# A graph network of two layers with experts: block sizes at the end of the second layer, expert steps in the attention's last ticks, and the side of memory of one buffer pool

## The chip, the cores and the metric

The kernel runs on one core of a Trainium2 chip. Its engines are TensorE (PE, with weight loads shown apart as PEld), VectorE (DVE), ScalarE (ACT), GpSimd (POOL) and SyncE (SP, which issues most transfers here). The metric is the device time of one execution in microseconds; several runs are taken and the median is compared.

## The reference

Four stages follow one another. Each takes the layer norm of `x` and adds its result to `x`. There are N = 6250 nodes with D = 256 values each, and 106,250 edges sorted by destination.

```python
# L0_gnn: a message for every edge, the mean by destination, then a second projection
h = relu(concat([x[src], edge_attr], 1) @ W1 + b1)
agg = segment_sum(h, dst, N) / maximum(segment_sum(1, dst, N), 1)[:, None]
x = x + relu(concat([x, agg], 1) @ W2 + b2)

# L0_ffn: graph attention over 131,072 other edges and one loop per node gives a score for
# each of 4 experts; the best 2 are mixed
h = (x @ W_gat).reshape(N, 4 heads, 4 experts)
e = leaky_relu(a_src[src2] + a_dst[dst2]);  alpha = segment_softmax(e, dst2)
agg = segment_sum(h[src2] * alpha[..., None], dst2) + b_gat
scores = layernorm(agg).reshape(N, 4, 4).mean(1);  w = softmax(top_k(scores, 2))
x = x + sum over ei of gate[ei] * (gelu(x @ W1[ei] + b1[ei]) @ W2[ei] + b2[ei])   # 256 -> 512 -> 256

# L1_gnn: h squared is gathered, summed with edge weights, and its root taken
h = relu(x @ Wp.T + bp)
agg = sqrt(segment_sum(edge_weight[:, None] * (h ** 2)[src], dst, N))
x = x + h @ W1.T + b1 + agg @ W2.T + b2

# L1_ffn: one shared network of three layers, and the best 2 of 4 small ones (256 -> 128 -> 64 -> 256)
gates = softmax(x @ gW + gb);  topw = softmax(top_k(gates, 2))
x = x + shared(x) + sum of topw * expert(x)
```

(In every line on the right the layer norm of `x` stands for `x`.)

## The kernel before

**Data.** The nodes are cut in T = 49 tiles of 128. The tile `x_all` holds `x` for all nodes through the whole kernel, and `b_all` the transposed normalized values, which are the matmuls' moving operand. All data are 32-bit floats. Each engine works through its own instructions in the order in which the program writes them; the framework adds the waits. So the order of the Python code is the order of every engine, and the loops below interleave several pieces of work by hand. Pieces are written as Python generators: one call of `next` writes one step, up to the next `yield`.

**Memory pools.** Tiles come from pools, which are laid from the left end of the on-chip memory (SBUF) or, with `side="right"`, from its other end. A pool that is closed gives its place to pools opened later, and then the first use of the new tile waits for the last use of the old ones. `ea1` (L1285) holds three buffers of edge attributes of 6144 bytes a partition, filled by `load_attr` on the queue SP (L1304). It lies at the left end, at bytes 153,856 to 172,288 of each partition, and the scratch of layer 1 behind it. `w5` and `n5`, opened at the right end for the first experts, hold their weights (bytes 207,520 to 226,016) and their hidden and output values (195,232 to 207,520). They cover scratch of layer 1: its hidden values and projections (172,288 to 210,176) and its sums (210,176 to 222,532).

**Layer 1, edges.** Groups of six tiles of 128 edges: gathers of `y` rows by POOL (L1101), transposes of the attributes, a projection, sums over destinations by matmuls with 0/1 matrices.

**Attention with the first experts.** The attention's edges stand in 640 columns of 128, eight to a tick, so there are NA = 80 ticks, and a loop of NA + 5 in which a tick's gathering, scoring, weighing, spreading and adding are each one step behind the other. `experts1` (L1540) is a generator of 396 steps. A step is eight matmuls with 256 columns: the first or second half of a hidden layer (`first`, with the Gelu at L1593), or one node tile's output (`second`, L1609 and the store to DRAM at L1613). Its weights come by `load` (L948) and its bias by L1569, both through SP, in whose order small loads at L941, L948, L1569 and their neighbours stand ahead of them. Each tick calls `slot()` five times. A slot writes one expert step (`advance(layers, n)`), one step of each routing or node job that stands ready (`run(steps, False)`), the loads of expert outputs (`load_outputs`, L1941) and the start of new jobs (`start_steps`). The fifth slot gives an expert step in ticks 0 to 69 alone:

```python
                slot(int(k < 70))
```

By that the 396 steps are used up in tick 81 of 85.

**Drain.** As the sums of attention become final, `gates` (L1840) turns them into routing weights, a chain of small DVE and ACT operations (Sqrt, Exp); `node_values` (L1953) mixes the four experts' outputs, normalizes, transposes, projects, squares and writes the row of `hp_dram` that layer 2 gathers. The loop behind the ticks writes what is left of all of these. Where it interleaves, ACT has to load the table of a function that it did not use last (L1719 and others).

**Layer 2.** When `hp_dram` is written, POOL gathers 831 tiles of 128 edges (L1101, `hg`), in 139 groups of six. `weights_of` (L2386) makes the matrices of edge weights, `add_up` (L2402, L2407) sums by matmul into one PSUM tile a block. A block is a run of node tiles, at most BT = 4:

```python
        blocks = [(t, BT) for t in range(0, T - 5, BT)] + [(T - 5, 2), (T - 3, 1), (T - 2, 2)]
```

When a block's last edge is summed, `roots` takes the square roots (L2419), `end_of2` ends each of its node tiles (projection, norm, transposes, logits of the gate; L2228), `gates2` (L2256) ranks the experts and `experts2` (L2310) computes the shared network and the four small ones: 11 calls of `first`, `then` and the like for the whole block, then per node tile three PSUM tiles of outputs, which DVE adds to `x_all` with the gate's weights; a DMA at L2369 writes the block out. The main loop (L2431 to L2452) makes one pass a group: it issues the gathers of nine groups ahead, writes matrices and sums, up to two steps of `experts2`, a step of each tile's end, and in every second pass starts a new tile's end. Only past the last group does every pass start one. The logits of two blocks have room beside each other in `px` (`area`). Between the drain and the layer DVE sets constants: the ones behind `g2_0` and `g2_1` (L2198), the zeros of `nothing` (L2220), and the small tiles `lower`, `place` and `second` (L2206 to L2214), which `gates` has of its own (L1828 to L1837).

After layer 2 a few instructions check that the graph fitted the fixed layout, and a general version, which did not run here, would be used otherwise.

Of the kernel before, what the change touches and what calls it, by code (L numbers as in the profile page):

```python
# [8 lines left out]
F32 = mybir.dt.float32  # L9
# [832 lines left out]
def kernel(ctx: ExitStack, tc: tile.TileContext, a: dict, out: bass.AP):  # L842
# [71 lines left out]
    with ExitStack() as fast:  # L914
# [275 lines left out]

        att = fast.enter_context(tc.tile_pool(name="att", bufs=1))
        gate = att.tile([P, T, X], F32, name="gate")
        attention = fast.enter_context(ExitStack())
        gat = attention.enter_context(tc.tile_pool(name="gat", bufs=1))
        src2 = gat.tile([P, KA], I32, name="src2")
# [82 lines left out]
        with ExitStack() as layer:  # L1278
# [3 lines left out]
            order = srt.tile([P, KT], F32, name="order")  # L1282
            wp = layer.enter_context(tc.tile_pool(name="w1", bufs=1))
            wix = layer.enter_context(tc.tile_pool(name="wix", bufs=1))
            wea = layer.enter_context(tc.tile_pool(name="ea1", bufs=3))  # L1285

            def load_weights():
                return (
# [347 lines left out]
        def advance(queue, n):  # L1636
            for _ in range(n):
                if queue and next(queue[0], queue) is queue:
                    queue.pop(0)
# [3 lines left out]
        with (  # L1643
# [180 lines left out]
                    )  # L1824
                    V.tensor_add(acc[:, :, at], acc[:, :, at], rest)


            lower = n2.tile([P, X, X], F32, name="lower")  # L1828
            V.memset(lower, 0.0)
            for k in range(1, X):  # L1830
                V.memset(lower[:, k, 0:k], 1.0)
            place = n2.tile([P, X], F32, name="place")
            for k in range(X):
                V.memset(place[:, k : k + 1], float(X - 1 - k))
            second = n2.tile([P, 2], F32, name="second")
            V.memset(second[:, 0:1], 0.0)
            V.memset(second[:, 1:2], 1.0)  # L1837
            bg = bcast_row(n2, "bg", a["L0_ffn_b_gat_T"])
            gamma = bcast_row(n2, "gamma", a["L0_ffn_ln_gamma_T"])
            beta = bcast_row(n2, "beta", a["L0_ffn_ln_beta_T"])  # L1840
# [246 lines left out]
                    steps.append([node_values(ws), False])  # L2087

            def slot(n=1):
                advance(layers, n)  # L2090
                run(steps, False)
                load_outputs()
                start_steps()
# [5 lines left out]
            def complete(t1):  # L2099

                while ends and ends[0] <= t1:
                    waiting.append((passed[0], ends[0] - passed[0]))
                    passed[0] = ends.pop(0)

            passed = [0]
            last_columns = list(range(KB, KT, G))
            counted = False
            for k in range(NA + 5):
                if k < NA:
                    fetch(k)  # L2110
                if k == 1:
                    own_edges()
                now, here, there, before = k - 2, k - 3, k - 4, k - 5
                if 0 <= before < NA:
                    add_up(before, 0)
                slot()
                if now in range(NA):
                    score(now, 0)
                slot()
                if here in range(NA):  # L2120
                    weigh(here)
                tables()
                if there in range(NA):
                    spread_out(there, 0)
                run(routing, False)
                slot()
                if 0 <= before < NA:
                    add_up(before, 1)
                slot()
                if now in range(NA):  # L2130
                    score(now, 1)
                run(routing, False)
                slot(int(k < 70))
                if there in range(NA):
                    spread_out(there, 1)
                for _ in range(2):
                    if last_columns:
                        count_last(last_columns.pop(0))
                if not last_columns and not counted:
                    routing.append([last_edges(), False])  # L2140
                    counted = True
                if counted and 0 <= before < NA:
                    complete(near_blocks(before + 1)[0] if before + 1 < NA else T)
            while layers or steps or routing or waiting or done["begun"] < T:
                slot()
                tables()
                run(routing, False)
# [4 lines left out]


        BT = 4
        blocks = [(t, BT) for t in range(0, T - 5, BT)] + [(T - 5, 2), (T - 3, 1), (T - 2, 2)]
        with (
            tc.tile_pool(name="w8", bufs=1, side="right") as wp,
            tc.tile_pool(name="e7", bufs=2) as wk,
# [36 lines left out]
            )  # L2195
            g2s = [wp.tile([EH2 + 1, NX, BT, P], F32, name=f"g2_{i}") for i in range(2)]
            for g2 in g2s:
                V.memset(g2[last, :, :, :], 1.0)  # L2198

            NQ = BT * NX  # L2200
            px = psx.tile([P, P + 8 * NQ], F32, name="px")
            lanes = px[:, 0:P]
            V.tensor_copy(lanes, lane)

            lower = wp.tile([P, NX, NX], F32, name="lower")
            V.memset(lower, 0.0)  # L2206
            for k in range(1, NX):
                V.memset(lower[:, k, 0:k], 1.0)
            place = wp.tile([P, NX], F32, name="place")
            for k in range(NX):  # L2210
                V.memset(place[:, k : k + 1], float(NX - 1 - k))
            second = wp.tile([P, 2], F32, name="second")
            V.memset(second[:, 0:1], 0.0)
            V.memset(second[:, 1:2], 1.0)  # L2214

            def area(at, n):
                return px[:, P + at : P + at + n]

            nothing = wp.tile([P, BT * P], F32, name="nothing")
            V.memset(nothing, 0.0)  # L2220

            def end_of2(b, i, root):


                w = blocks[b][0] + i
                pm = psm.tile([P, D], F32, name="pt")
                mm(pm, lambda c: root[:, i, :], lambda c: w2t, 1)
                V.tensor_add(x_all[:, w, :], x_all[:, w, :], pm)  # L2228
                st = wk.tile([P, 6], F32, name="ln_st")
                V.bn_stats(st, x_all[:, w, :])  # L2230
                mv = wk.tile([P, 2], F32, name="ln_mv")
                V.bn_aggr(mv, st)
                rs = wk.tile([P, 1], F32, name="ln_rs")
                V.tensor_scalar(rs, mv[:, 1:2], EPS, None, op0=OP.add)
                SC.activation(rs, rs, AF.Sqrt)
                yield
                V.reciprocal(rs, rs)
                off = wk.tile([P, 1], F32, name="off")
                V.tensor_scalar(off, mv[:, 0:1], rs, -1.0, op0=OP.mult, op1=OP.mult)
                xn = wk.tile([P, D], F32, name="xn")  # L2240
                SC.activation(xn, x_all[:, w, :], AF.Identity, bias=off, scale=rs)
                yield
                transposed(psm, b_all[:, w, :], xn)
                yield
                pg = psm.tile([P, D], F32, name="pt")
                mm(pg[:, 0:NX], lambda c: b_all[:, w, c * P : (c + 1) * P], lambda c: gw[:, c, :])
                V.tensor_add(area(b % 2 * NQ + i * NX, NX), pg[:, 0:NX], gb)

            def gates2(b):


                t0, n = blocks[b]
                q = n * NX
                s = area(b % 2 * NQ, q).rearrange("p (n k) -> p n k", k=NX)
                m = wk.tile([P, BT], F32, name="m")[:, :n]
                V.tensor_reduce(m, s, axis=AX.X, op=OP.max)  # L2256
                V.tensor_sub(s, s, m.unsqueeze(2).to_broadcast([P, n, NX]))
# [44 lines left out]
                    gate[:, t0 : t0 + n, :], pick.rearrange("p n i k -> p n k i"),  # L2302
                    axis=AX.X, op=OP.add,
                )

            def experts2(b):

# [32 lines left out]
                for e in range(NX):  # L2340
                    if e + 1 < NX:
                        first(e + 1)
                        yield
                    then(e)
                    yield
                for i in range(n):
                    t = t0 + i
# [71 lines left out]
                SC.activation(root, pe, AF.Sqrt)  # L2419
                return [(b, i, root) for i in range(n)]  # L2420

            complete, ends, coming, routes, layers = [], [], [], [], []
            ended = [0] * len(blocks)
            AHEAD = 9
            for k in range(AHEAD):
# [3 lines left out]
            while k < len(groups2) or complete or coming or ends or routes or layers:  # L2429
                if k + AHEAD < len(groups2):  # L2430
                    fetch(k + AHEAD)  # L2431
                if k + 1 < len(groups2):
                    weights_of(k + 1)
                if k < len(groups2):
                    add_up(k)
                advance(layers, 1)
                for item in list(ends):
                    if next(item[1], ends) is ends:
                        ends.remove(item)
                        b = item[0]  # L2440
                        ended[b] += 1
                        if ended[b] == blocks[b][1]:
                            routes.append(gates2(b))
                            layers.append(experts2(b))
                if coming and (k % 2 or k >= len(groups2)):
                    b, i, root = coming.pop(0)
                    ends.append((b, end_of2(b, i, root)))
                while complete:
                    coming += roots(complete.pop(0))
                advance(routes, 1)  # L2450
                advance(layers, 1)
                k += 1  # L2452


# [69 lines left out]
```

## Time and profile before

| what | value |
|---|---|
| median of 3 runs | 3698.01 us (3695.89 to 3698.55) |
| profiled execution | 3697.09 us, its span 3695.1 us |
| mean granted clock of TensorE | 0.897 |
| busy: PE / PEld / DVE / ACT / POOL | 3433.4 / 2766.9 / 2199.3 / 1406.3 / 2252.5 us |
| POOL's gathers for the attention (L1101, `sg`) | 640, 612.7 us |
| POOL's gathers for layer 2 (L1101, `hg`) | 831, 784.1 us |
| expert matmuls of the attention stage (L1088, `ph` and `py`) | 1600 and 1568, 386.8 and 384.8 us |

The profile is of one execution, so its sums belong to its own 3697.09 us. A busy time is that of all instructions of an engine; instructions that only issue a transfer, wait or branch are not counted. The granted clock is the share of full speed that TensorE had, and a matmul's duration stretches with it. A row of the timeline names the engine, the line of the kernel, the operation, `out<-in` by the program's names, and in brackets the idle time ahead with what released it. A mean over the span hides that the stages have different limits, so stretches of the span are read apart.

### The profile page before, as it was taken

What the parts mean: (1) busy time and instruction counts of PE and PEld (TensorE: products, weight loads), DVE (VectorE), ACT (ScalarE), POOL (GpSimd) and SP (SyncE); (2) the same over time, 40 slices, a digit from 0 to 9 for tenths busy, and PEclk for the clock granted to TensorE, in tenths of its full rate; (3) what the DMA queues carried; (4) which work ended last, traced back from release to release, by engine and by line L of the source; (5) the groups of instructions that cost most, each with busy time, mean ns of one, the idle gap of its engine ahead of it and who ended that gap; (6) DMA issues with size and microseconds to landing.
All of it is one profiled execution on the core that took longest, in us unless ns stands there. A gap on an engine that the chain in (4) does not pass through costs nothing. (4 is left out here: it accounts for less than half of the span.)

```text
span 3695.1 us, 54304 instructions
## 1 busy us (share of the span) xinstructions
PE 3433.4 (93%) x18495; PEld 2766.9 (75%) x18495; DVE 2199.3 (60%) x6073; ACT 1406.3 (38%) x2714; POOL 2252.5 (61%) x2364
## 2 busy tenths in 40 slices
PE   7899999999999999899999999996678889888898
PEld 3678888888888887788888888895455566666675
DVE  9999984444444444687757576877233444444445
ACT  4444444444444443334544454654011222211214
POOL 0466666666666664666655555560777777777771
PEclk9999999999999999999999999997557776776668
DMA  5456656656555553443534343543222222222221
GB/s 170 131 173 177 181 174 175 181 177 176 176 177 179 173 176 111 124 96 89 133 82 125 81 125 86 144 93 88 53 53 59 59 59 59 59 59 59 59 59 29
DMA packets 298963, 428.30 MB, mean 116 GB/s; under 512 B 101495, under 2 KB 208774, under 8 KB 298679
## 3 DMA queue, kind: packets, MB, share of 16 engines
q1 hardware_dynamic: 201254, 244.98, 22.0%
q0 software_dynamic: 89408, 178.08, 19.1%
q8 instruction: 150, 2.46, 0.3%
q10 hardware_dynamic: 8016, 1.68, 0.2%
q14 instruction: 135, 1.10, 0.1%
HBM read 382.05 MB, written 42.49 MB: 115 GB/s over the span
## 5 line engine op out<-in xcount | busy, mean ns | idle before, releaser
L1101 POOL DMA_INDIRECT yg<-y_dram,src x882 | 854.3, 969 | 590.2 <-issue 225.8
L1101 POOL DMA_INDIRECT hg<-hp_dram,src x831 | 784.1, 944 | 339.6 <-issue 235.2
L1101 POOL DMA_INDIRECT sg<-gat_dram,src x640 | 612.7, 957 | 402.3 <-DVE px L1729 170.0
L1088 PE MATMUL ph<-w1b,et 128*128 128x256 f32 x3528 | 835.3, 380 | 0.0
L1088 PEld LDWEIGHTS ph<-w1b,et 128*128 128x128 f32 x3528 | 636.8, 190 | 68.5
L2407 PEld LDWEIGHTS pe<-eq,hg 128*128 128x128 f32 x1984 | 398.8, 272 | 282.8 <-issue 141.6
L2407 PE MATMUL pe<-eq,hg 128*128 128x96 f32 (+10 forms) x1984 | 447.3, 364 | 161.3 <-DMA hg<-hp_dram,src 127.1
L1406 DVE TENSOR_TENSOR yg<-ph,yg 128x512 f32<-128x512 f32 x441 | 303.6, 688 | 384.5 <-PE ph L1088 381.9
L1088 PE MATMUL ph<-b_all,w 128*128 128x256 f32 (+1 forms) x1600 | 386.8, 381 | 11.2 <-DMA w<-in_L_ffn_W_dram 11.2
L1088 PE MATMUL py<-w,hh 128*128 128x256 f32 x1568 | 384.8, 384 | 7.7 <-ACT hh L1593 7.7
L1411 ACT ACTIVATE h<-yg 128x512 f32<-128x512 f32 x441 | 276.6, 628 | 293.1 <-DVE yg L1406 280.9
L2386 DVE TENSOR_SCALAR eq<-px,dst,ew 128x96 f32<-128x96 f32 x831 | 256.9, 369 | 175.3 <-PE pe L2407 123.6
L1083 ACT ACTIVATE et<-pt 128x512 f32<-128x512 f32 x441 | 262.5, 596 | 240.6 <-PE pt L1082 229.4
L1088 PEld LDWEIGHTS ph<-b_all,w 128*128 128x128 f32 x1600 | 291.8, 191 | 44.1 <-issue 11.3
L1088 PEld LDWEIGHTS py<-w,hh 128*128 128x128 f32 x1568 | 287.1, 190 | 42.5 <-ACT hh L1593 10.1
L1593 ACT ACTIVATE hh<-ph,b 128x256 f32<-128x256 f32 (+1 forms) x400 | 166.2, 466 | 296.7 <-PE ph L1088 295.8
L1082 PE MATMUL pt<-ident,ea 128*128 128x128 f32 x1764 | 269.5, 275 | 3.3 <-ACT et L1083 3.3
L1757 PE MATMUL po<-pp,B 128*128 128x240 f32 (+10 forms) x1280 | 254.9, 338 | 2.5 <-DVE B L1745 1.6
L1082 PEld LDWEIGHTS pt<-ident,ea 128*128 128x128 f32 x1764 | 213.9, 143 | 48.1 <-issue 19.4
L1757 PEld LDWEIGHTS po<-pp,B 128*128 128x128 f32 x1280 | 217.3, 191 | 15.2 <-issue 1.7
L1088 PE MATMUL py<-ew,g 65*128 65x256 f32 x392 | 165.7, 555 | 0.3 <-DVE some L2476 0.3
L1736 DVE TENSOR_TENSOR pp<-px,A 128x960 f32<-128x960 f32 (+10 forms) x160 | 156.0, 975 | 3.6 <-PE po L1757 3.3
(337 smaller groups left out, 4456.1 us busy)
## 6 DMA issues: line engine op xcount, KB each, us to landing
ea<-in_edge_attr_dram SPq DMA_DIRECT2D x147, 768.0 KB
y<-y SPq DMA_DIRECT2D x196, 128.0 KB
w<-in_L_ffn_W_dram SPq DMA_DIRECT2D x48, 512.0 KB
y<-ys SPq DMA_DIRECT2D x96, 256.0 KB
rb<-low_dram SPq DMA_DIRECT2D x80, 256.0 KB
yg<-y_dram,src POOLq DMA_INDIRECT x882
hg<-hp_dram,src POOLq DMA_INDIRECT x831
sg<-gat_dram,src POOLq DMA_INDIRECT x640
```

Of the source, the lines that this page charges most:

```text
L1082: TE.transpose(pt[:, c, :], src[:, c * P : (c + 1) * P], ident)
L1083: SC.activation(dst, pt.rearrange("p c k -> p (c k)"), AF.Copy)
L1088: TE.matmul(dst, lhs(c), rhs(c), start=c == 0, stop=c == n - 1)
L1101: GP.indirect_dma_start(out=dst, out_offset=None, in_=table[0:NP, :], in_offset=IndirectOffsetOnAxis(ap=idx, axis=0),)
L1406: V.tensor_add(y, ph, y)
L1411: SC.activation(h[:, j : j + 2, 0:D], y, AF.Relu)
L1593: SC.activation(hidden[u][:, f, :n, :], ph[:, f - f0, :n, :], AF.Gelu, bias=b1[:, e, f : f + 1],)
L1736: V.tensor_tensor(pps[g, half][:, :, 0:n, :], pay[:, js, :].unsqueeze(2).to_broadcast([P, HG, n, HV]), near[g][:, js, 0:n].unsqueeze(3).to ...
L1757: TE.matmul(po.rearrange("p b v -> p (b v)"), B[:, j, :], pp[:, j, 0:n, :].rearrange("p b v -> p (b v)"), start=half == 0 and j == 0, stop ...
L2386: V.tensor_scalar(equals[k][:, j, :], lanes[:, 0:NW], dst_of[:, t : t + 1], ew[:, t : t + 1], op0=OP.is_equal, op1=OP.mult,)
L2407: TE.matmul(sums[b][:, lo - t0 * P : hi - t0 * P], hg[:, j, :], eq[:, j, lo - n0 : hi - n0], start=False, stop=after >= (t0 + n) * P,)
```

## The change

Three things are changed.

First, `ea1` goes to the right end of the memory, at bytes 205,696 to 224,128. What lay behind it at the left end moves down by 18,432 bytes. The weights of the first experts then lie over `ea1` (and a table of counts) instead of layer 1's scratch, and their hidden and output values over layer 1's sums.

Second, slots: a slot gives an expert step if its `n` is not zero and the tick is below 80, or if it is the first of its tick, or if it lies in the loop behind the ticks. The fifth slot gives one in ticks 0 to 61 instead of 0 to 69. Counted from the loop: ticks 62 to 69 give four steps instead of five, tick 80 one instead of four, ticks 81 to 84 one each; 387 of the 396 are written by the end of the ticks and nine in the loop behind.

Third, layer 2. Blocks: ten of 4, then three of 2 (from tiles 40, 42 and 44) and three of 1 (46, 47, 48); before, eleven of 4, then 2, 1 and 2. A pass of the main loop writes up to three steps of `experts2` instead of two, and a tile's end is started in every pass once the tiles are those of the small blocks. As a block's `experts2` can now be ahead of its `gates2`, its outputs are held back until the routing is written, and the logits of four blocks have room. The ones and zeros of `g2` and `nothing` are set by POOL instead of DVE, and `lower`, `place` and `second` once, at the start, for both layers.

```diff
@@ in the pool att, ahead of layer 1
+        lower = att.tile([P, X, X], F32, name="lower")
+        V.memset(lower, 0.0)
+        for k in range(1, X):
+            V.memset(lower[:, k, 0:k], 1.0)
...
+        second = att.tile([P, 2], F32, name="second")
...
-            wea = layer.enter_context(tc.tile_pool(name="ea1", bufs=3))
+            wea = layer.enter_context(tc.tile_pool(name="ea1", bufs=3, side="right"))
...
             def slot(n=1):
-                advance(layers, n)
+                if n and (k < NA or k == NA + 5 or slots[0] % 5 == 0):
+                    advance(layers, n)
+                slots[0] += 1
                 run(steps, False)
...
-                slot(int(k < 70))
+                slot(int(k < 62))
...
+            k = NA + 5
             while layers or steps or routing or waiting or done["begun"] < T:
                 slot()
...
-        blocks = [(t, BT) for t in range(0, T - 5, BT)] + [(T - 5, 2), (T - 3, 1), (T - 2, 2)]
+        small = T - T % BT - 2 * BT
+        blocks = [(t, BT) for t in range(0, small, BT)]
+        blocks += [(t, 2) for t in range(small, T - 3, 2)] + [(t, 1) for t in range(T - 3, T)]
...
-                V.memset(g2[last, :, :, :], 1.0)
+                GP.memset(g2[last, :, :, :], 1.0)
...
-            px = psx.tile([P, P + 8 * NQ], F32, name="px")
+            px = psx.tile([P, P + 10 * NQ], F32, name="px")
...
+            def logits(b):
+                n = blocks[b][1] * NX
+                return area((0, NQ, 8 * NQ, 9 * NQ)[b % 4], n)
...
-            V.memset(nothing, 0.0)
+            GP.memset(nothing, 0.0)
...
+                routed.add(b)        # at the end of gates2
...
+                while b not in routed:   # in experts2, ahead of the outputs
+                    yield
...
-                if coming and (k % 2 or k >= len(groups2)):
+                if coming and (k % 2 or coming[0][0] * BT >= small):
...
                 advance(routes, 1)
-                advance(layers, 1)
+                advance(layers, 2)
```

More of the change, by code (lines that the diff above doesn't have):

```diff
@@ L1192 @@
         gate = att.tile([P, T, X], F32, name="gate")
+        lower = att.tile([P, X, X], F32, name="lower")
+        V.memset(lower, 0.0)
+        for k in range(1, X):
+            V.memset(lower[:, k, 0:k], 1.0)
+        place = att.tile([P, X], F32, name="place")
+        for k in range(X):
+            V.memset(place[:, k : k + 1], float(X - 1 - k))
+        second = att.tile([P, 2], F32, name="second")
+        V.memset(second[:, 0:1], 0.0)
+        V.memset(second[:, 1:2], 1.0)
         attention = fast.enter_context(ExitStack())
@@ L1825, in last_edges @@
                     V.tensor_add(acc[:, :, at], acc[:, :, at], rest)
[L1828 to L1837, printed above, removed]
             bg = bcast_row(n2, "bg", a["L0_ffn_b_gat_T"])
@@ L2103, in complete @@
                     passed[0] = ends.pop(0)
-            passed = [0]
+            passed, slots = [0], [0]
             last_columns = list(range(KB, KT, G))
@@ L2197 @@
             for g2 in g2s:
-                V.memset(g2[last, :, :, :], 1.0)
+                GP.memset(g2[last, :, :, :], 1.0)
             NQ = BT * NX
-            px = psx.tile([P, P + 8 * NQ], F32, name="px")
+            px = psx.tile([P, P + 10 * NQ], F32, name="px")
             lanes = px[:, 0:P]
             V.tensor_copy(lanes, lane)
[L2205 to L2214, printed above, removed]
             def area(at, n):
                 return px[:, P + at : P + at + n]
+            def logits(b):
+                n = blocks[b][1] * NX
+                return area((0, NQ, 8 * NQ, 9 * NQ)[b % 4], n)
             nothing = wp.tile([P, BT * P], F32, name="nothing")
-            V.memset(nothing, 0.0)
+            GP.memset(nothing, 0.0)
             def end_of2(b, i, root):
@@ L2246, in end_of2 @@
                 mm(pg[:, 0:NX], lambda c: b_all[:, w, c * P : (c + 1) * P], lambda c: gw[:, c, :])
-                V.tensor_add(area(b % 2 * NQ + i * NX, NX), pg[:, 0:NX], gb)
+                V.tensor_add(logits(b)[:, i * NX : (i + 1) * NX], pg[:, 0:NX], gb)
             def gates2(b):
@@ L2253, in gates2 @@
                 q = n * NX
-                s = area(b % 2 * NQ, q).rearrange("p (n k) -> p n k", k=NX)
+                s = logits(b).rearrange("p (n k) -> p n k", k=NX)
                 m = wk.tile([P, BT], F32, name="m")[:, :n]
@@ L2420, in roots @@
                 return [(b, i, root) for i in range(n)]
-            complete, ends, coming, routes, layers = [], [], [], [], []
+            complete, ends, coming, routes, layers, routed = [], [], [], [], [], set()
             ended = [0] * len(blocks)
```

## The prediction

> **What bounds the kernel now.** The page first: TensorE is nominally busy for nearly the whole span, so that figure decides nothing. The busy times by stretch do (their columns: stretch, its length, busy time of PE, weight loads, DVE, ACT and POOL with instruction counts, granted clock, DMA share, GB/s).
>
> ```profile
> PE 3433.4 (93%) x18495; PEld 2766.9 (75%) x18495; DVE 2199.3 (60%) x6073; ACT 1406.3 (38%) x2714; POOL 2252.5 (61%) x2364
> ```
>
> ```profile
> 1457.00:1489.10 32.10, 15.40 (x70) 12.18 (x68) 16.79 (x70) 6.40 (x14) 4.96 (x6) 0.75 0.21 44
> 2381.00:2533.00 152.00, 148.71 (x1100) 134.23 (x1096) 110.92 (x327) 87.91 (x159) 71.14 (x74) 0.99 0.42 93
> 2533.00:2547.20 14.20, 0.00 (x0) 0.00 (x0) 12.93 (x50) 2.50 (x6) 0.00 (x0) 0.50 0.70 190
> 2533.00:2580.70 47.70, 20.90 (x85) 14.16 (x85) 37.91 (x146) 18.81 (x47) 0.00 (x0) 0.68 0.45 124
> 3500.00:3618.00 118.00, 112.04 (x428) 88.96 (x427) 54.30 (x195) 21.17 (x38) 89.23 (x95) 0.64 0.23 62
> 3620.40:3687.10 66.70, 65.03 (x279) 42.69 (x277) 39.29 (x169) 36.57 (x74) 0.00 (x0) 1.00 0.05 16
> ```
>
> There are six stages. Edges, layer 1, to 1457: PE full. A gap to 1489: PE idle 16.7 of 32.1 us. Attention with experts to 2533: PE full at clock 0.99, DVE 73%. A drain to 2580.7: a serial chain, PE idle for its first 14.2 us. Layer 2: POOL issues 831 gathers at a pitch of 1.247 us (0.94 busy, 0.30 issue), 1036 us that nothing here alters. A tail from 3620.4, where the last sum is taken, to 3687.1: PE 65.0 of 66.7 us at clock 1.00; 8 us of output and end follow. The change touches the gap, the drain and the tail.
>
> **Gap: attribute buffers at the right end.** The timeline of the queue SP and of PE:
>
> ```profile
> 1302.85 126.35 SPq L1304 DMA_DIRECT2D ea<-in_edge_attr_dram  x15
> 1479.02 0.35 SPq L941 DMA_DIRECT2D bg<-in_L_ffn_b_gat_T_dram  x1
> 1483.59 2.56 SPq L948 DMA_DIRECT2D w<-in_L_ffn_W_dram  x2
> 1489.13 5.83 PE L1088 MATMUL ph<-b_all,w 128*128 128x256 f32 x16 [11.19 <-DMA w<-in_L_ffn_W_dram]
> ```
>
> SP has nothing to do from 1429 to 1479, yet the experts' first weights are issued at 1483.6. Their buffers share memory with layer 1's scratch, whose last user is the final node's projection at 1478.9. After the change those addresses are held by the edge attributes, last read at 1456.8. Issue to use took 1489.1 - 1483.2 = 6 us, so expert steps could start at 1463. All 16.7 idle us lie behind that, and the first 16 matmuls took 5.83 us where 1.73 us for 8 is usual: 2.4 us more. So the gain is at most 19 us, and 0 if SP's order keeps the weights behind its nine small loads. Against the full 19: the hidden activations overlie layer 1's sums (read until 1469.8), and attention's first score matmul, now at 1509.75, has its rows only at 1498.5, so it moves up 11 us. I take -12. PE is full for the next 1040 us, which carries it on. Expert steps that come between layer 1's last four PE steps can delay the attention's gathers by 4 x 1.73 = 7 us; 640 gathers at 1.247 are 798 us of that 1040, which covers it. Uncovered it would be 7.
>
> **Drain: fewer expert steps.** The experts take 396 steps of 1.73 us (8 matmul passes; 0.87 for the first halves of the single tile 48). Before, they end in tick 81 of 85. After, ticks 62 to 69 give four instead of five, tick 80 one instead of four, ticks 81 to 84 one each: 387 are issued by the end, and nine (seven full, two half: 13.8 us) go into the loop behind. As PE bounds these ticks, the last attention sum comes 14 us earlier (10 if DVE's 73% begins to bind, 17 if the ticks' waits fill too). The nine must then lie beside the drain. It has 26.8 us of idle PE, so the time itself is covered; uncovered it would be 13.8. Their outputs go by DRAM to nodes 44 to 48: the last store lands some 3 us after the last step, about where attention ended before, and those sums begin at 2555 now; with the drain 12 earlier that is still 7 us of slack.
>
> Not covered is ScalarE's table. Four of the nine steps use Gelu among Sqrt and Exp, two loads each:
>
> ```profile
> 2498.18 0.23 ACT L1719 ACTIVATE z<-z 128x32 f32<-128x32 f32 x1
> 2498.43 1.28 ACT L1593 ACT_TABLE_LOAD   x1
> ```
>
> Eight by 1.28 is 10.2 us on an ACT that is busy 18.8 of 47.7; four transposes and projections may each wait one step, 7 more. I take +6 of 0 to +17, nearer the low end, since half the loads fall where ACT waits for DVE.
>
> A rule speaks against this step. The Trainium skill (ScalarE: Activation LUTs, What ACT_TABLE_LOAD costs) prices a switch at 1.28 us plus a 1.38 us pipeline drain. By it eight would be 21 us and the drain's gain nearly gone. The rows above leave 0.02 us between the end of one function and the load for the next, so the trace shows the load alone.
>
> Two memsets leave DVE:
>
> ```profile
> 2533.08 0.18 DVE L1909 TENSOR_REDUCE top<-pick 128x8 f32<-128x32 f32 x1
> 2533.74 1.76 DVE L2198 MEMSET g<- 1x2048 f32 x1 [0.48 <-issue]
> 2535.54 0.16 DVE L1910 TENSOR_TENSOR mu<-top 128x4 f32<-128x4 f32 x1
> 2536.26 1.76 DVE L2198 MEMSET g<- 1x2048 f32 x1 [0.48 <-issue]
> 2538.06 0.17 DVE L1914 TENSOR_SCALAR top<-mu 128x4 f32<-128x4 f32 x1
> ```
>
> Both sit inside the routing chain: each holds its successor some 2 us. That is -4 (at worst -1, if the next wait swallows it). On POOL they and the 0.48 us zero block stand in front of the gathers, behind the experts' end; POOL is idle from 2480 to the first gather at 2580. No row shows such a memset on POOL; between DVE's 4.0 us in all and twice that they fit, and what they could cost DVE lies between 0 and +3; I take 0, as DVE works while POOL issues gathers all through layer 2. The ten small memsets (0.06 to 0.07 us) that now run once fit DVE's 3.8 us wait for the first DMA at the start. The drain: -14 + 6 - 4 = -12, between -21 and +10.
>
> The Trainium skill (GPSIMD Engine Reference, 1. Specifications) says POOL shares its SBUF interface with VectorE and contends with instructions of two SBUF inputs, which the drain's node sums are. By it up to the whole memset time could return; no row here shows it.
>
> **Tail: smaller blocks, three expert steps a pass.** I stepped through the loop over 139 gather groups and listed which step is issued in which pass. Prices at full clock come from the chain of waits:
>
> ```profile
> 3643.70 1.73 PE py L1088 x8
> 3665.10 0.67 PE ph L1088 x6
> 3671.61 4.49 PE ph L1088 x20
> 3676.74 1.44 PE ph L1088 x6
> ```
>
> A call is two matmuls: eight with 256 columns took 1.73 us, so a call takes 0.43 us for two tiles, 0.86 for four and 0.22 for one (six with 128 columns: 0.67). A block takes 18 calls, and each tile then 5 output calls of 0.43 = 2.15. A tile's node end (projection, transposes, gate) is 1.3. Before, with the last sum, 14 calls of block 40 to 43 are left: 12.0 + 8.6; blocks 44-45: 12.0; 46: 6.1; 47-48: 12.0; 4.5 node ends: 5.9. Sum 56.6, and 66.7 were taken: 10 us of waits, 5 of them in the last block, with nothing to fill them. After: 10 calls of block 42-43 and its outputs: 8.6; 44-45: 12.0; three single tiles: 18.3; 2.5 ends: 3.3. Sum 42.2. Waits grow with single tiles (1.43 us an expert alone against 0.65 of work): 12. So 54, a gain of 12. The moved work lies in passes 125 to 138: by the same prices 61 us of PE work become 75 in 105 us. At the granted 0.64 only 67 fit, and 8 would run over; from 0.72 up, nothing. PE was busy 112 of 118, so a clock that follows load is likely; I take 1 over. Tail -11, between -2 and -17. The wait for routing before the outputs is order, not an instruction: in the list it delays one pass per large block.
>
> **Sum.** -12 - 12 - 11 = -35. The profiled execution took 3697.09 us, 2.0 outside its span of 3695.1, and 0.9 under the median 3698.01. 3698 - 35 = 3663.
>
> **Rivals.** (a) The weights do not move up: SP's order is fixed when the program is compiled, and nothing in this trace proves that they go ahead of the small loads. Gap 0: 3675. Speaking against: layer 2's weights were issued at 2533, before node loads of 2540 that stand earlier in the code. (b) The clock stays at 0.64 in the dense passes: tail -3: 3671. For it: the row 3500 to 3618. (c) Slower: the last ticks are bound by DVE's chain, not by PE (ticks 82 to 84 already are: PE 10.9 of 20 us from 2520 to 2540). Then nothing comes earlier, and the nine steps are added to the drain with their loads: 13.8 + 10.2 - 4 = +20. With gap and tail at half, 3698 + 20 - 11.5 = 3706. It decides once those two bring under 13. Against it: PE is at 20.00 of 20 us in every stretch from 2400 to 2500. (d) The pieces hold at their weak ends and cancel: 3698 less 2 to 6.
>
> **How the numbers follow.** Forecast 0.48, (a) 0.17, (b) 0.13, (c) 0.13, (d) 0.09. A measurement tells about 0.2%, 7.4 us, from no change. Faster: 0.48 + 0.17 + 0.13 = 0.78; same 0.09; slower 0.13. The range runs from the good ends taken nearly together (3698 - 55 = 3643) to where (a) meets a drain of no gain and a tail at half (3698 - 6 = 3692); beyond lie (c) and part of (d).
>
> **What would show it.** Right: expert weights on SP before 1465 and PE without its 11 us wait; the last attention sum at about 2507 (2533 less 12 and 14) and the first gather near 2557 (2580.7 less 24), 831 gathers still at 1.247; from last sum to last output 55 us. Wrong: weights still behind the small loads; an ACT row of many loads in the drain with the first gather no earlier than the gap's gain; a last sum that comes more than 3 us after the last gather has landed.

## The result, and the profile after

The changed kernel takes 3648.32 us (median of 4, 3644.53 to 3657.15) against 3698.28 us before (median of 4): a ratio of 0.9869, 95% interval 0.985 to 0.9888, or 50 us less where 35 were forecast. The time lies inside the range of 3643 to 3692. The profiled execution has a span of 3647.9 us, 47.2 less than before.

Two things in the description of the kernel are not so. It says that the order of the Python code is the order of every engine. The profile before already showed otherwise: the ones of `g2`, which stand behind the drain's loop in the code, ran inside the routing chain. So an instruction of a later piece can stand ahead of earlier ones, and a step's place is read from the trace alone. And what it calls layer 1's sums is, by the code, the pool of the two buffers `h` that the sums' matmuls read.

The stretches that were read before, in the kernel after (length, busy time of PE, weight loads, DVE, ACT, POOL with instruction counts, granted clock, DMA share, GB/s). The second is the drain, the third the last 60 us of the gathers, the fourth the tail:

```profile
1457.00:1489.10 32.10, 29.70 (x152) 25.56 (x151) 15.47 (x58) 16.11 (x30) 3.89 (x5) 1.00 0.44 122
2498.90:2544.90 46.00, 31.84 (x149) 23.00 (x147) 34.42 (x132) 24.82 (x57) 4.10 (x4) 0.92 0.50 142
3520.90:3580.90 60.00, 60.00 (x280) 52.28 (x280) 27.79 (x107) 14.41 (x31) 45.30 (x49) 0.72 0.23 62
3584.20:3638.70 54.50, 52.89 (x278) 38.88 (x276) 36.99 (x173) 29.50 (x75) 0.00 (x0) 1.00 0.06 20
```

PE is now busy for 29.7 of the gap's 32.1 us instead of 15.4, and for 31.8 us of the drain instead of 20.9. The queue SP in the kernel after:

```profile
1428.42 0.35 SPq L1315 DMA_DIRECT2D ea<-in_edge_attr_dram  x1
1456.41 0.38 SPq L1580 DMA_DIRECT2D b<-in_L_ffn_b_dram  x1
1456.84 1.88 SPq L948 DMA_DIRECT2D w<-in_L_ffn_W_dram  x2
1480.31 0.34 SPq L941 DMA_DIRECT2D bg<-in_L_ffn_b_gat_T_dram  x1
```

The experts' weights go out at 1456.8 instead of 1483.6, now ahead of the small loads (`bg` is the first of them), 28 us after the last load of attributes. The chain of waits in the drain, in the kernel after (start, length, what; its longest engine pieces around the moved steps and the constants):

```profile
2502.31 2.63 PE ph L1088 x16
...
2507.02 1.28 ACT L1604
...
2509.66 2.71 PE py L1088 x8
...
2513.23 1.28 ACT L1964
...
2515.02 1.28 ACT L1912
...
2522.64 3.55 POOL g L2203 x2
2526.24 0.54 POOL nothing L2218
2526.82 3.32 PE pe L2403 x4
```

The moved expert matmuls are in the chain, and so are three table loads of ScalarE (1.28 us each). The round trip of the outputs by DRAM is not. POOL wrote the ones in 3.55 us and the zeros in 0.54. The first matmuls of layer 2, which need the zeros, stand in PE's queue ahead of the last nodes' transposes, and PE waited 3.60 us for them, so POOL's writes are in the chain as well.

Landmarks of all profiles that can be compared. "First sum" is the start of the first matmul of attention's sums (`po`), "to last sum" the time from there to the start of the last one, "drain" from there to the first gather of layer 2, "tail" from the last gather's start to the end of the span. The 831 gathers between took 1036 us in each, in e11 1039 and in e12 1037.

| kernel | first sum | to last sum | drain | tail | span |
|---|---|---|---|---|---|
| before | 1541.3 | 991.2 | 48.4 | 78.2 | 3695.1 |
| changed | 1524.4 | 973.7 | 46.8 | 67.0 | 3647.9 |
| e1, attributes alone | 1528.4 | 990.2 | 48.1 | 80.6 | 3683.3 |
| e2, slots alone | 1541.4 | 976.1 | 51.5 | 79.5 | 3684.7 |
| e3, layer 2 alone | 1541.0 | 990.7 | 48.2 | 62.6 | 3678.5 |
| e4, constants alone | 1544.8 | 990.3 | 45.7 | 78.2 | 3695.0 |
| e9, changed, constants back | 1528.2 | 975.3 | 50.4 | 67.8 | 3657.7 |
| e10, changed, old blocks | 1525.2 | 974.2 | 47.9 | 60.8 | 3644.1 |
| e11, changed, Relu at the end | 1522.0 | 977.7 | 47.7 | 62.5 | 3648.8 |
| e12, e10 with 8 more steps moved | 1523.2 | 965.3 | 58.5 | 60.1 | 3644.4 |

By stage the change brought 16.9 us ahead of attention's first sum, 17.5 in its ticks, 1.6 in the drain and 11.2 in the tail.

### The profile page after: what moved, and what is told of

Read it like the earlier page. It is cut to its first block, busy times and chain, and to the rows that moved or that the text cites. A ratio compares the mean times of both kernels' runs of the same rounds, so it can differ in the third digit from the quotient of the medians.

```text
span 3647.9 us, 54596 instructions
## 1 busy us (share of the span) xinstructions
PE 3417.3 (94%) x18623; PEld 2768.4 (76%) x18623; DVE 2196.7 (60%) x6104; ACT 1418.2 (39%) x2748; POOL 2257.6 (62%) x2367
## 4 chain that ended last, share of the span: by engine, by line
PE 63%; POOL 15%; issue 9%; DVE 6%; DMA 5%; ACT 1%; SPq 0%; DVEq 0%; POOLq 0%; ACTq 0%
PE ph L1088 29%; POOL hg L1101 14%; PE py L1088 10%; PE pt L1082 6%; PE po L1768 5%; PE pe L1435 4%; PE pe L1441 3%; DMA hg<-hp_dram,src 3%; PE pt L1088 2%; PE pe L2408 1%; DMA rb<-low_dram 1%; PE pa L1705 1%; DVE junk L979 1%; DVE key L1249 1%; POOL yg L1101 1%
## 5 line engine op out<-in xcount | busy, mean ns | idle before, releaser
L2408 PE MATMUL pe<-eq,hg 128*128 128x96 f32 (+15 forms) x2036 | 464.4, 365 | 162.0 <-DMA hg<-hp_dram,src 133.0
```

Of the source, the lines that this page charges most:

```text
L2408: TE.matmul(sums[b][:, lo - t0 * P : hi - t0 * P], hg[:, j, :], eq[:, j, lo - n0 : hi - n0], start=False, stop=after >= (t0 + n) * P,)
```

## The experiments

**Each part alone (e1 to e4).** The edits are the change's own lines, one part at a time, on the kernel before.

```diff
e1: wea = ... tc.tile_pool(name="ea1", bufs=3, side="right")
e2: slot() with its condition, slot(int(k < 62)), k = NA + 5
e3: blocks, logits, routed, coming[0][0] * BT >= small, advance(layers, 2)
e4: lower, place, second in att; GP.memset for g2 and nothing
```

> Only the attribute buffers go to the right end; everything else as before. Theory (the three parts are independent and add up): the experts' first weights are issued near 1456 us, the first attention sum moves from 1541.3 to about 1524.4, and these 17 us reach the end unchanged: first gather of layer 2 at about 2564, tail from last gather to end of span 78 us as before, total about -17. Rival (the drain or the last ticks swallow part of what comes early): first sum 17 us earlier, first gather less than 12 us earlier.

Measured: 3685.27 us against 3697.97, ratio 0.9964 (0.995 to 0.9978). The weights were issued at 1457.9 and the first gather came at 2566.6, 14.3 us earlier, so what comes early is kept. But the first sum moved by 12.9 us, not by the 16.9 of the whole change, and the time by 12.7 instead of 17.

> Only the slots of the last ticks are changed (387 instead of 396 expert steps before the end of the ticks). Theory: nothing before tick 62 moves; the last attention sum, 2532.5 before, comes 17 us earlier (2515); the drain behind it, 48.4 us before, gets 2 to 4 us longer by three more table loads; total -13 to -15. Rival (VectorE's chain bounds the last ticks, so that the nine steps only move): last sum less than 5 us earlier, total 0 to +10.

Measured: 3687.13 us, ratio 0.9967 (0.9953 to 0.9982). The last sum came 15.0 us earlier (17 expected), the drain grew by 3.1, and the time fell by 10.8, less than the 13 to 15 expected. PE bounds the ticks; the rival is out.

> Only layer 2's blocks, its three expert steps a pass and its logits are changed; the constants stay on VectorE. Theory: first gather at 2580.9 as before, 831 gathers at 1.247 us, the stretch from the last gather to the end of the span shortens from 78.2 us to 67, total -11. Rival (the tail's gain needed the higher clock that the stretch before the tail had in the changed kernel, 0.74 against 0.60 to 0.68): -3 to -6.

Measured: 3684.03 us, ratio 0.9963 (0.9949 to 0.9978). The tail shortened by 15.6 us in the profile and the median by 14: more than the tail of the whole change. The profiled execution is the fastest of the five. Its clock in the last 60 us of the gathers was 0.91, so it does not decide the rival.

> Only the constants are moved: ones and zeros of layer 2 set by POOL instead of VectorE, the three small tables once at the start. Theory: the drain, 48.4 us from last attention sum to first gather before, loses the 4 us that the two memsets held the routing chain; total -4. Rival (the loads of expert outputs that end next in the same chain take it up): -1 to 0.

Measured: 3697.62 us, ratio 0.9996 (0.9987 to 1.0006). The drain lost 2.7 us of the 4 that the theory gives, but the first sum came 3.5 later, and the time did not change. Within that, the weights were issued 1.2 us later and PE's first expert matmul came 2.9 later (1492.0 against 1489.1). Why is not settled.

Together the four medians give 38 us less, the whole change gives 50.

**Which memory do the weights wait for? (e5)** The changed kernel with the two expert pools opened in the other order:

```diff
-        w5 = experts.enter_context(tc.tile_pool(name="w5", bufs=2, side="right"))
         n5 = experts.enter_context(tc.tile_pool(name="n5", bufs=2, side="right"))
+        w5 = experts.enter_context(tc.tile_pool(name="w5", bufs=2, side="right"))
```

> The changed kernel, with the two expert pools opened in the other order, so that the weights lie over layer 1's sums (their memory is last read near 1469) and the hidden values over the attribute buffers; nothing else differs. Theory (the last use of the memory under the weights sets when they are issued): weights issued near 1470 instead of 1456.8, first expert matmuls after 1475, first attention sum near 1534 instead of 1524.4, total 8 to 11 us more than the changed kernel. Rival (the side of the attribute buffers itself, or SP's order, is what counts): within 2 us of the changed kernel.

The chip of e5 to e8 ran the kernel before in 4351.92 us, so only places within a trace and ratios are read from them. Ratio 0.9979 (0.9964 to 0.9993). PE, and then SP, in e5:

```profile
1630.22 2.87 PE L1441 MATMUL pe<-h,eq 128*128 128x257 f32 x12 [0.19 <-ACT h L1422]
```

```profile
1633.23 0.38 SPq L1580 DMA_DIRECT2D b<-in_L_ffn_b_dram  x1
1633.66 1.55 SPq L948 DMA_DIRECT2D w<-in_L_ffn_W_dram  x2
```

The last read of layer 1's `h`, which the weights now cover, ends at 1633.1. The bias, which leads the weights on SP and lies over `h` too, goes out at 1633.2. In e7, with the pools as changed, the same last matmuls on `h` ran from 1645.1 to 1647.9, but the bias and the weights went out from 1634.7, the moment when the last transposes of attributes ended, 13 us ahead of the end of those matmuls. PE, and then SP, in e7:

```profile
1634.08 0.60 PE L1082 MATMUL pt<-ident,ea 128*128 128x128 f32 x4
```

```profile
1634.71 0.38 SPq L1580 DMA_DIRECT2D b<-in_L_ffn_b_dram  x1
```

The attribute buffers are on the right in both. What counts is the last reader of the memory under the weights. What the delay costs, 8 to 11 us by the theory, stays open: the changed kernel itself did not run on this chip.

**The constants (e6, e9).** The changed kernel with `g2` and `nothing` set by DVE and the small tables set twice, as before.

> The changed kernel, with the constants as before (ones and zeros on VectorE, the three small tables twice). The four parts alone summed to -38 us, all together to -50, and most of the 12 us lie ahead of the first attention sum. Theory I (the constants are worth what they were alone): first attention sum at 1524, drain 3 us longer, total +1 to +4 against the changed kernel. Theory II (with the weights early, VectorE's queue at the start of attention counts, and the ten small memsets in it hold the first sums back): first attention sum near 1528, drain +3 to +5, total +7 to +10.

Ratio 0.9957 (0.9936 to 0.9978), not comparable with the changed kernel for the reason given. Its drain of 50.0 us (46.5 to 47.9 in e5, e7 and e8) agrees with the repeat:

> The same kernel as e6 (the changed kernel with the constants as before), again, since the chip of e6 ran every kernel some 17% slower and its stages cannot be set beside those of the changed kernel. Theory I (the constants are worth what they were alone): first attention sum at 1524, drain 50 us, total +1 to +4 against the changed kernel. Theory II (with the weights early the ten small memsets in VectorE's queue hold the first sums back): first attention sum near 1528, drain 50, total +7 to +10.

Measured: 3658.13 us, ratio 0.9891 (0.9875 to 0.9908), 9.8 us above the changed kernel's median; the two intervals overlap a little. The size and the first sum (1528.2) are those of theory II. Whether its cause holds is read from DVE and PE of e9 at the start of attention; the last line is a piece of its drain's chain:

```profile
1482.09 0.07 DVE L1829 MEMSET lower<- 128x16 f32 x1
1489.39 0.43 DVE L1931 TENSOR_TENSOR b<-b,xn 128x256 f32<-128x256 f32 x1 [2.79 <-DMA xn<-in_L_gnn_b_dram]
```

```profile
1493.82 0.37 PE L1781 MATMUL py<-q,b 128*128 128x49 bf16 x8 [2.75 <-DVE q L1775]
```

```profile
2542.30 1.77 DVE g L2203
```

The ten small memsets are back among DVE's operations from 1482.1 to 1483.7, and PE waits 2.75 us for DVE's `q` (2.20 in e1, where the memsets stand there too); in the changed kernel no such wait stands at that place. But between the memsets and this `q` DVE itself waits 2.79 us for a load, `xn`, as it does in the changed kernel (2.63), so the trace does not show that the memsets hold `q` back. From the issue of the weights to the first sum e9 takes 69.8 us and e1 70.5, the changed kernel 67.6, e10 67.9, e11 66.0 and e12 66.9. Part of this is the clock: a run of 16 expert matmuls behind that `q` took 5.22 us in e9 and 6.06 in e1, at granted clocks of 0.70 and 0.60, but 4.24 in the changed kernel (0.87) and 3.72 in e11 and e12 (1.00). And on the chip of e5 to e8 the same stretch took 112.3 us in e6, 112.5 in e7 and 111.9 in e8, which have no memsets there. So the first sum comes later with the constants back, but why is not shown.

In the drain a memset of 1.77 us is in the chain again, and the drain is 3.6 us longer (50.4 against 46.8). Of the 9.8 us these 3.6 alone have a cause that the traces show. Of the rest, 2.2 us lie between the weights and the first sum, 1.6 ahead of the weights, 1.6 in the ticks and 0.8 in the tail.

**The third step and the blocks (e7, e8, e10).** e7 takes the third step away and keeps the new blocks; e8 and e10 take the new blocks away and keep the third step.

```diff
e7:
-                advance(layers, 2)
+                advance(layers, 1)
e8, e10:
-        blocks = [(t, BT) for t in range(0, small, BT)]
-        blocks += [(t, 2) for t in range(small, T - 3, 2)] + [(t, 1) for t in range(T - 3, T)]
+        blocks = [(t, BT) for t in range(0, T - 5, BT)] + [(T - 5, 2), (T - 3, 1), (T - 2, 2)]
```

> The changed kernel, with two expert steps a pass in layer 2 as before, on the new blocks. Theory (by the list of passes, TensorE work of 52 us instead of 42 is left when the last gather is done): the stretch from the last gather to the end of the span is 77 us instead of 67, total +10. Rival (TensorE is full in the last 60 us of the gathers anyway, so what is issued earlier only waits): +0 to +4.

> The changed kernel, with the old blocks (eleven of 4, then 2, 1, 2) and three steps a pass. Theory (the work left decides; by the list of passes it is 36 us instead of 42): the tail is 4 to 6 us shorter than in the changed kernel, total -5. Rival (a last block of two tiles cannot be filled, and the larger blocks come ready later, so waits take the place of work): tail 3 to 8 us longer.

Ratios 0.9973 (0.995 to 0.9996) and 0.9931 (0.9909 to 0.9953). On that chip the last sum came 64 to 68 us after the last gather in all four kernels, so the tail decides nothing there, and two steps on the new blocks stay untried on the other chips. The old blocks were run again:

> The same kernel as e8 (the changed kernel with the old blocks and three steps a pass), again, for the same reason. Theory (the work left decides, 36 us by the list of passes instead of 42): the stretch from the last gather to the end of the span is 61 to 63 us instead of 67. Rival (a last block of two tiles leaves TensorE waiting): 70 to 75.

Measured: 3645.09 us, ratio 0.9857 (0.984 to 0.9873), with a tail of 60.8 us: 6.2 less than in the changed kernel, as the list of passes gave. The last 60 us of e10's gathers have nearly the clock that the changed kernel had in its own (0.72):

```profile
3523.40:3583.40 60.00, 58.19 (x239) 44.33 (x238) 27.73 (x102) 13.97 (x28) 45.33 (x49) 0.74 0.24 62
```

Four profiles with the new blocks have tails of 62.5 to 67.8 us, two with the old ones and the third step 60.1 and 60.8. The old blocks without the third step had 78.2 to 80.6 (before, e1, e2, e4). It helps to split the tail at the last sum, the last matmul of `pe` on `hg`. What lies ahead of it, from the last gather's start, is called the lag.

| profiles | lag | from the last sum to the end |
|---|---|---|
| old blocks, two steps: before, e1, e2, e4 | 4.0 to 4.8 | 73.9 to 75.8 |
| new blocks, three steps: changed, e3, e9, e11 | 10.6, 6.1, 11.4, 6.0 | 56.4 to 56.6 |
| old blocks, three steps: e10, e12 | 6.7, 3.9 | 54.0, 56.3 |

So the third step, with a tile's end in every pass, brings the tail's gain: some 18 us behind the last sum, where the clock was 1.00 before (3620.4 to 3687.1) and in the changed kernel (3584.2 to 3638.7) alike. That the smaller blocks give some of it back is likely, but not shown: behind the last sum they take 0.1 to 2.6 us more, and the lag differs by 5 us between executions of the same layer 2. e10 is the best median of all, but its interval overlaps that of the changed kernel.

**ScalarE's table (e11).**

```diff
-                        hidden[u][:, f, :n, :], ph[:, f - f0, :n, :], AF.Gelu,
+                        hidden[u][:, f, :n, :], ph[:, f - f0, :n, :],
+                        AF.Relu if u >= len(units) - 2 else AF.Gelu,
```

> The changed kernel, with Relu in place of Gelu in the experts' last two units (nodes of tiles 46 to 48), so that the four moved hidden steps need no table of their own; the outputs of those tiles differ. Theory (the switches of ScalarE's table lie on the drain's chain): three loads fewer of 1.28 us, drain 42 to 43 us instead of 46.8, last attention sum as in the changed kernel. Rival (the chain goes through the moved matmuls and the round trip of their outputs by DRAM, ScalarE has slack): drain 46 to 47.

Measured: 3648.57 us, ratio 0.9868 (0.9851 to 0.9884). Three table loads behind the last sum instead of six, as before the change, and a drain of 47.7 us, against 46.8 in the changed kernel and 47.9 in e10, which has the same drain. Three of the loads stand in the changed kernel's chain, but without them the drain is no shorter, so the theory is out. In the chain of e11 the moved matmuls still stand; the round trip by DRAM, the rival's other half, stands in neither chain.

**More steps moved (e12).** e10 with `slot(int(k < 54))`.

> The kernel of e10 (old blocks, three steps a pass, everything else as changed) with the fifth slot's step given in ticks 0 to 53 instead of 0 to 61: eight more expert steps go behind the ticks, 17 in all. Theory (TensorE is full in the ticks to the last one, and behind them the last expert output now sets the end): last attention sum 12 to 14 us earlier than in e10 (2486 instead of 2499), drain 12 to 16 us longer, total -1 to +4 against e10. Rival (the drain still has room): drain less than 6 us longer, total -8 or better.

Measured: 3647.2 us, ratio 0.9869 (0.9852 to 0.9885). The last sum came 10.9 us earlier than in e10 (2488.5), the drain was 10.6 us longer, each a little less than expected, and the time is 2.1 us more. The theory holds: the gain is used up. With 17 steps behind the ticks the last expert matmul starts at 2525.0 (2520.1 in e10) and the gathers start where they did. Here the round trip of the outputs by DRAM does stand in the drain's chain.

## Why the prediction was right, point by point

- **Gap, -12 between -19 and 0: -16.9.** The mechanism is the one named, and e5 shows it: the first expert matmul ran at 1465.1 (1463 forecast). The size is the term that failed: it let attention's first score matmul, 11 us earlier at most, set the gain. That matmul came 13.6 us earlier (1509.77 before):

```profile
1496.19 1.09 PE L1705 MATMUL pa<-part,rb 128*128 128x8 bf16 x38
```

PE had expert steps to fill the time, and its idle time from the last read of the attributes (1457) to the first sum fell from 17.6 of 84.3 us to 3.4 of 67.6. Alone (e1) the part was worth 12.9. The other 4 came only where the constants were moved too, in a way that is not shown. The attention's gathers started 1.4 us later (1484.4), within the 7 that were allowed for, and the 1040 us behind covered it.
- **Ticks, -14 between -10 and -17: -17.5**, and -15.1 alone (e2). Seven full and two half steps at 1.73 us, on a full PE, were the right account. The changed kernel gained 2.4 more than the part alone and half a microsecond more than the range allowed; why is open. Rival (c), DVE as the bound, is out.
- **Tables, +6 of 0 to +17: nothing.** This step failed. Only three loads more appeared, not eight, since neighbouring Gelus shared one, and e11 takes three away without a gain, though three stand in the changed kernel's chain. The Trainium skill (ScalarE: Activation LUTs, What ACT_TABLE_LOAD costs) adds a pipeline drain of 1.38 us to a load; an estimate by it was 21 us for eight loads. The changed kernel's trace has no room for that drain: a load that starts at 2505.41 and takes 1.28 us is followed at 2506.70 by the function that needs it.
- **Memsets, -4 (at worst -1).** The drain shortened by 2.7 alone (e4) and by 3.6 in the changed kernel (against e9). That POOL's writes and the matmuls that need its zeros would come into the chain, from 2522.6 to 2530.1, was not in the prediction. Nor was it that the first sum comes later with the constants back (e9).
- **POOL and DVE.** The Trainium skill (GPSIMD Engine Reference, 1. Specifications) says that the two contend where DVE reads two operands from SBUF. While POOL wrote, from 2522.64 to 2526.77, single node sums took 0.45 to 0.48 us (2523.28, 2524.34, 2524.81); without POOL they took 0.45 to 0.49 (2505.81 to 2510.75). The drain shows no contention with these writes, and the value 0 was right.
- **Tail, -11 between -2 and -17: -11.2.** That the sum is so near is luck: two terms were wrong, and they cancel. The dense passes were to run over by 1 us; the lag grew by 6.6, from 4.0 to 10.6, at a clock of 0.72 in the 60 us ahead. That is what the text had named as a sign of being wrong, and rival (b) had named a low clock as the cause, but the text expected nothing to run over from 0.72 up. Behind the last sum 12 us were to be gained, and 17.8 were (74.2 to 56.4): the last output matmul ended 47 us after the last sum instead of 54, so the 12 us of waits that the single tiles were given were too many. How much of the lag is the clock can only be argued from profiles of the same layer 2. Up to the last sum, counted from 60 us ahead of the last gather, PE did 335 or 336 pieces in all four of them. e3 had a lag of 6.1, with this clock in the last 60 us:

```profile
3555.90:3615.90 60.00, 54.18 (x307) 46.40 (x306) 29.13 (x113) 17.32 (x36) 45.29 (x49) 0.91 0.24 62
```

PE did 307 pieces in 54.2 us there and 280 in 60.0 in the changed kernel. e11 had 6.0 at 0.80. e9 had 0.89 in its last 60 us and yet a lag of 11.4, but there the clock fell behind the last gather, from its start to the last sum:

```profile
3589.90:3601.30 11.40, 11.40 (x33) 7.47 (x32) 4.94 (x20) 1.92 (x6) 0.94 (x1) 0.55 0.13 35
```

The clock alone was not varied, so its share, up to some 5 us, is argued and not shown.
- **Sum.** The four measured stages give 47.2, the estimates 35. The 12 us between are 5 in the gap, 3.5 in the ticks and 3.6 in the drain. (The medians differ by 50: the profiled execution is slower than the median of its kernel.) The last sum of attention came at 2498.1 (2507 forecast) and the first gather at 2544.9 (2557 forecast). So the time lies inside the range, but the gain was forecast too small, and mostly in two terms, the gap's size and the table loads. Rivals (a), (c) and (d) are out; (b) is right in that the clock made passes run over, and wrong in the tail that it gave.

## What to carry to other kernels

A load that is issued late with an idle queue may wait for the last reader of the memory under its buffer: look at what lay there, and put it under something that dies early. Work moved from a stage that one engine fills into a drain with idle time is free only until its own outputs set the drain's end; from there on it is an exchange of one for one. A part that is worth nothing alone can look otherwise in the whole: the constants brought 0.4 us alone, and leaving them out cost 9.8. So try parts by leaving each out as well, and then ask where the time lies: only 3.6 of these 9.8 us have a cause that the traces show. Where a term comes out right, look at its pieces: the tail's 11 us were two errors of some 6 us each.

## What the runs showed of the hardware

The granted clock in the last 60 us of the gathers differed between executions of the same layer 2: 0.72 (changed), 0.80 (e11), 0.89 (e9) and 0.91 (e3). A busy PE did not keep it up: in the changed kernel PE was busy for all of the 20 us from 3520.9 at a clock of 0.50. A memset of 1 x 2048 values takes POOL 1.77 us, as long as DVE (1.76).

On the chip of e5 to e8 the engines were hardly slower at their work: DVE was busy for 2192.7 us in e7 and 2196.7 in the changed kernel on its chip, PE for 3498.1 and 3417.3. But some of PE's instructions came late, with nothing that the profile shows to wait for. PE in e7:

```profile
1706.41 0.17 PE L1705 MATMUL pa<-part,rb 128*128 128x12 bf16 x1 [2.62 <-issue]
1709.21 0.17 PE L1705 MATMUL pa<-part,rb 128*128 128x12 bf16 x1 [2.63 <-issue]
```

Against the changed kernel e7 takes 223 us more up to the first sum (its weights went out at 1635.1 instead of 1456.8), 245 in the ticks, 1 in the drain, 162 in layer 2's gathers and 56 in the tail. The kernel before took 18% more on this chip than on that of e1 to e4. Why is open.
